# Moving relation gathers from the first pass of a graph network to the expert tiles that follow it

## The chip, the cores and the metric

One Trainium2 chip, one core. The time is the device time of one execution in microseconds (us). Each kernel is also profiled once; durations below come from that one profiled execution.

## The reference

Four blocks run one after the other on 3125 nodes of 256 features, in float32.

- Block 1 is a graph network of three layers. A layer takes, for every node, the mean over the edges that end in it (103125 edges, loops among them), multiplies by two weight matrices, and normalizes.
- Block 2 is a mixture of 16 experts. Each node picks its two best experts by a gate; an expert is relu(x w1 + b1) w2 + b2 with 512 hidden units, and the two answers are added to the node by their weights.
- Block 3 is a relational graph network: a message is the source's row times the row of the edge's relation. There are 500 relations, whose rows of 256 features carry a gate value as a 257th.
- Block 4 is a mixture of 8 experts with 1024 hidden units.

Only one thing of block 3 matters here: its relation rows depend on the edges' types alone, so they can be fetched in any earlier block.

## The kernel before

Nodes are held as 25 blocks of 128 (NB = 25). The edges of a block are sorted into 26 tiles of 128 edges, so there are 650 edge tiles in all.

**Pass 1** is the first layer of block 1, and it also sorts the edges. It is a loop of 28 steps (L640 to L662), each of which works on four blocks at different stages: `load` and `rank` of block i (the win loads on SP, L518, then a long chain between VectorE, DVE for short, and TensorE, PE: kb L528, prior L534, upto L542, place L546, ri L549), `permute` and `lay` of block i - 1 (held L593, main L605, the edge types into main_t L611), `build` of block i - 2 (one-hots L507, PE products, the store of cells on SP L637), and the sums (L359, L362) and `finish` of block i - 3. Passes 2 and 3 (from L848 and L873) are the second and third layers, which read the stored cells.

**The relation rows** of block 3 are fetched in advance from the 500-row table r_rows. `fetch_relations(n, after)` takes the next n of 217 groups of three edge tiles each (the last has two). For a group it does one small DVE operation (L296) that copies the types of its tiles into the tile paced and reads a piece of `after`, so that the group cannot start before that data is there; then three indirect DMAs of 128 rows of 257 numbers on POOL (L300) into a rel_rows tile, of which there are four; and it issues the store of the group before on SP (L311), into r_seq in HBM. Block 3 reads r_seq from there. The calls stand in this order:

- pass 1: at the end of `rank` (after qi, from the third block on), after `lay`, before `build` and after `finish`, one group each: 95 groups, 285 gathers
- pass 2 and pass 3: two groups in each of 25 steps, 100 groups
- ten groups ahead of block 2 (L1179), and the remaining twelve behind its expert tiles in the program's text (L1182), with beta as the data that they wait for. Since beta is there early, a scheduler that orders each engine's instructions has put nearly all of them ahead of the first tile.

**Block 2** is the function `moe` (L908 to L1170) with the tag f0. The routing part works out for each expert tile of 256 rows which nodes it takes (tok_g, tok_s), with which weight (wt_q) and by which expert (exp_i). Then 34 expert tiles run. Tile t reads its expert's number on SP (the value_load at L1100, 34 in all), loads w1_t and w2_t on SP (three buffers each), and has its 256 rows gathered by two indirect DMAs on POOL (xt, L249, issued two tiles ahead, eight buffers). PE transposes them (pt, L1110), multiplies by w1_t (ph, L1125), and after the activation (L1130 on DVE, L1134 on ScalarE) by w2_t (py, L1143). DVE scales (y, L1146, eight buffers), and two indirect DMAs on POOL add y to f0_total in HBM (L1148). At the end of tile t the function `beside(t)` of the caller is called; before, it adds beta to block t of xs.

Each engine runs its instructions in one order, and POOL and SP each issue their DMAs in that order: a gather or a store that waits holds what is behind it.

Of the kernel before, what the change touches and what calls it, by code (L numbers as in the profile page):

```python
# [40 lines left out]
I32 = mybir.dt.int32  # L41
# [9 lines left out]
NB = 25  # L51
# [22 lines left out]
def bcast(ap, n):  # L74

    return bass.AP(tensor=ap.tensor, offset=ap.offset, ap=[[0, P], [1, n]])
# [3 lines left out]
def gnn_moe_kernel(  # L80
# [9 lines left out]
    nc = tc.nc  # L90
# [27 lines left out]
    xs = const.tile([P, NB, D], F32, name="xs")  # L118
# [169 lines left out]
    def fetch_relations(n, after):  # L288

        for i in islice(next_r, n):
            g = of_group[i]
            rows = stage.tile([P, RG, W], F32, name="rel_rows")
            types = paced[:, g[0]:g[-1] + 1]
            nc.vector.scalar_tensor_tensor(  # L296
                types, after[:, :len(g)], 0, main_t[:, g[0]:g[-1] + 1],
                op0=ALU.bitwise_and, op1=ALU.bitwise_or)
            for j, t in enumerate(g):
                nc.gpsimd.indirect_dma_start(  # L300
                    out=rows[:, j, :], out_offset=None, in_=r_rows,
                    in_offset=bass.IndirectOffsetOnAxis(ap=types[:, j:j + 1], axis=0))
            store_relations()
            landing.append((i, rows))

    def store_relations():
        if not landing:
            return
        i, rows = landing.pop()
        n = len(of_group[i])  # L310
        nc.sync.dma_start(r_seq[i], rows[:, :n, :].rearrange("p r w -> p (r w)"))  # L311
# [10 lines left out]
    with ExitStack() as block:  # L322
# [30 lines left out]
        def sums_of(b, cell, layer, psum, between={}):  # L353


            width = D + 1 if layer == 0 else D
            z = psum.tile([P, D + 1], F32, name="z", bufs=2)
            for sh in range(NB):
                nc.tensor.matmul(z[:, :width], cell[:, sh, :], part_lo[:, sh, :width],  # L359
                                 start=sh == 0, stop=False)  # L360
                for i in range(2):
                    nc.tensor.matmul(z[:, :D], cell[:, sh, :], part_hi[:, sh, i, :],  # L362
                                     start=False, stop=sh == NB - 1 and i == 1)
                if sh in between:
                    between[sh]()
            return z

        def finish(b, z, layer):
            if layer == 0:
                nc.vector.tensor_copy(raw_dst[:, b:b + 1], z[:, D:])  # L370
                deg = work.tile([P, 1], F32, name="deg")
                nc.vector.tensor_scalar(deg, z[:, D:], 1.0, None, op0=ALU.max)
                nc.vector.reciprocal(inv_dst[:, b:b + 1], deg)
            zt = work.tile([P, D], F32, name="zt")
            nc.vector.scalar_tensor_tensor(zt, z[:, :D], inv_dst[:, b:b + 1], own[:, b, :],
                                           op0=ALU.mult, op1=ALU.add)
            if layer < 2:
                nc.vector.scalar_tensor_tensor(h[:, b, :], zt, 0.0, h[:, b, :],
                                               op0=ALU.max, op1=ALU.add)
            else:  # L380
                xt = work.tile([P, D], F32, name="xt")
                nc.scalar.dma_start(xt, base[b * P:(b + 1) * P, :])
                nc.vector.tensor_add(zt, zt, h[:, b, :])
                nc.vector.scalar_tensor_tensor(xs[:, b, :], zt, sound[:, 0:1], xt, op0=ALU.mult,
                                               op1=ALU.add)
            return zt

        with ExitStack() as first:
# [123 lines left out]
            def load(b):  # L512

                win = steps.tile([P, 6, 2, WH], F16, name="win", bufs=2)
                for half in range(2):
                    c = 2 * b + half
                    at_tile = nc.sync.value_load(begin[0:1, c:c + 1], min_val=0, max_val=ET - WH)
                    nc.sync.dma_start(win[:, :, half, :], words[:, :, bass.ds(at_tile, WH)])  # L518
                return win
# [47 lines left out]
            def permute(b, win, slot, to):  # L567


                def two(a):  # L570
                    return a.rearrange("p h (t two) -> p (h t) two", two=2)

                n = WH // 2
                all_of = [P, 2 * n, NS, 2]
                hit = steps.tile(all_of, F16, name="hit", bufs=1)
                nc.vector.tensor_tensor(
                    hit, two(to)[:, :, None, :].to_broadcast(all_of),
                    iota_tile[:, None, :, :].to_broadcast(all_of), op=ALU.is_equal)
                put = steps.tile([P, 2 * n, 3, NS, 2], F16, name="put")
                for i in range(3):  # L580
                    nc.vector.tensor_tensor(
                        put[:, :, i, :, :], hit,
                        two(win[:, 1 + i, :, :])[:, :, None, :].to_broadcast(all_of), op=ALU.mult)
                ends = psum.tile([P, 2, 3, NS], F32, name="ends")
                for half in range(2):
                    oh = one_hots(two(slot)[:, half * n:(half + 1) * n, :], n, iota_0, P,
                                  "oh_slot", n)
                    for t in range(WH):
                        nc.tensor.matmul(ends[:, half, :, :], oh[:, t // 2, :, t % 2],
                                         put[:, half * n + t // 2, :, :, t % 2],  # L590
                                         start=t == 0, stop=t == WH - 1)
                held = steps.tile([P, 3, NS, 2], F16, name="held")
                nc.scalar.activation(held, ends.rearrange("p h i t -> p i t h"), AF.Copy)  # L593


                for t in range(2):
                    nc.scalar.activation(held[:, :, b + t, 1], ends[:, 1, :, b + 1 - t], AF.Copy)
                return held
# [42 lines left out]
            def words_of(held):  # L641
                return held.rearrange("p i t h -> p (i t h)").bitcast(I32)

            loaded, ranked, moved, built = {}, {}, {}, {}
            for i in range(NB + 3):
                if i < NB:
                    loaded[i] = load(i)
                    ranked[i] = rank(i, loaded[i])
                if 0 <= i - 1 < NB:
                    moved[i - 1] = permute(i - 1, loaded.pop(i - 1), *ranked.pop(i - 1))  # L650
                    lay(i - 1, moved[i - 1])
                    if i > 1:
                        fetch_relations(1, words_of(moved[i - 1]))
                if 0 <= i - 2 < NB:
                    if i > 2:
                        fetch_relations(1, words_of(moved[i - 2]))
                    built[i - 2] = build(i - 2, moved.pop(i - 2))
                if 0 <= i - 3 < NB:
                    z = sums_of(i - 3, built.pop(i - 3), 0, psum)
                    done = finish(i - 3, z, 0)  # L660
                    if i > 3:
                        fetch_relations(1, done.bitcast(I32))  # L662

        with ExitStack() as flags:
            one = flags.enter_context(tc.tile_pool(name="g0_deg0", bufs=1))
# [16 lines left out]
        with ExitStack() as slow:  # L682
# [8 lines left out]
            with tc.For_i(0, n_slow, 1):  # L691
# [32 lines left out]
                for layer in range(3):  # L724
# [4 lines left out]
                    for b in range(NB):  # L729
# [3 lines left out]
                        z = psum.tile([P, D], F32, name="ps", bufs=3)  # L733
# [17 lines left out]
        with ExitStack() as later:  # L751
# [96 lines left out]
            for b, cell in enumerate(ahead_of(load_cell, 2)):  # L848
                z = sums_of(b, cell, 1, psum,
                            {12: lambda: fetch_relations(1, places(b, psum))})  # L850
# [3 lines left out]
                done = finish(b, z, 1)  # L854
# [20 lines left out]
            for b, cell in enumerate(ahead_of(load_cell, 2)):  # L875
                choice = chosen(b - 1)
                step = lambda: next(choice, None)
                z = sums_of(b, cell, 2, psum, {13: step, 19: step} if b > 0 else {})
                next(packs[b])
                done = finish(b, z, 2)  # L880
# [294 lines left out]
    with ExitStack() as block:  # L1175
        keep = block.enter_context(tc.tile_pool(name="f0_tokens", bufs=1))
        beta = keep.tile([P, D], F32, name="beta")
        nc.scalar.dma_start(beta, bcast(f0_beta, D))
        fetch_relations(10, top_v[:, NB - 1, :].bitcast(I32))  # L1179
        moe("f0", 16, 512, f0_b1, f0_w1, f0_w2, f0_b2, AF.Relu, None, f0_x, f0_total, 34,  # L1180
            lambda t: t < NB and nc.vector.tensor_add(xs[:, t, :], xs[:, t, :], beta))
        fetch_relations(len(of_group), beta.bitcast(I32))  # L1182
        store_relations()
    rel_ctx.close()
# [7 lines left out]
    with ExitStack() as block:  # L1192
# [14 lines left out]
        with ExitStack() as prep:  # L1207
# [6 lines left out]
            for kern, w, name in ((km, g1_mwt, "mw"), (ku, g1_uwt, "uw")):  # L1214
# [4 lines left out]
                for bo in range(4):  # L1219
                    for bi in range(4):  # L1220
                        i, sign = blades[bo][bi]
# [259 lines left out]
```

## Time and profile before

| what | value |
|---|---|
| runs | 3075.04, 3080.94, 3124.3 us; median 3080.94 |
| profiled execution, its own time | 3081.72 us |
| its span | 3079.8 us |
| mean granted TensorE clock | 0.910 |
| PE, DVE, ACT, POOL busy | 81%, 57%, 14%, 51% |
| pass 1 | about 155 to 681 us |
| routing of block 2 | 1341 to 1460 us |
| expert tiles of block 2 | 1460 to 1741 us |
| relation gathers (L300) | 650, of 0.943 to 3.072 us each, median 0.949 |

Times in the profile count from the start of the span. Engines: PE is the matrix engine, PEld its weight loads, DVE the vector engine, ACT the scalar engine, POOL the engine that issues the indirect DMAs, SP the one that issues the plain ones. An arrow (<-) names what an instruction waited for; "issue" is time in which an engine waited for nothing that the profile shows. A line number is that of the kernel before; in the changed kernel the lines from L660 on are two lower up to the end of `moe`, and somewhat higher behind it.

### The profile page before, as it was taken

How to read it: one execution, taken by the hardware profiler on the slowest of the kernel's cores; microseconds unless marked ns; L12 is line 12 of the kernel's file. 1: busy time of each engine (PE TensorE's matmuls, PEld its weight loads, DVE VectorE, ACT ScalarE, POOL GpSimd, SP SyncE). 2: the span in 40 equal slices, each digit the busy share in tenths (PEclk: the TensorE clock that was granted, in tenths of full speed). 3: DMA queues.
4: the chain of work that ended last, by engine and by line, in shares of the span. 5: the costliest groups of instructions: out<-in, count | busy, mean ns of one | idle time of the engine just before them, and what ended most of it. 6: DMA issues, size and time to landing. Idle time of an engine off the chain costs nothing.

```text
span 3079.8 us, 47955 instructions
## 1 busy us (share of the span) xinstructions
PE 2499.6 (81%) x17712; PEld 1986.2 (64%) x17712; DVE 1767.9 (57%) x4734; ACT 434.1 (14%) x1119; POOL 1566.1 (51%) x1379
## 2 busy tenths in 40 slices
PE   1767766778888999942999518999999996899997
PEld 0356654654777588832788406777777775788886
DVE  6688886766455366662233377788888787111110
ACT  1321221223000210000111050000000000122221
POOL 1067776761455256675566316666666660333331
PEclk9888897789999999976999859999999997899998
DMA  7046665652666368865777537777777770665653
GB/s 222 3 143 190 182 185 175 185 187 81 203 220 226 123 217 276 265 192 159 207 200 194 118 136 261 241 244 248 249 249 251 240 221 19 220 184 175 187 172 96
DMA packets 294160, 581.12 MB, mean 189 GB/s; under 512 B 77946, under 2 KB 176955, under 8 KB 289939
## 3 DMA queue, kind: packets, MB, share of 16 engines
q1 hardware_dynamic: 207459, 389.64, 36.9%
q0 software_dynamic: 76992, 177.86, 23.3%
q10 hardware_dynamic: 9456, 10.36, 1.1%
q8 instruction: 146, 2.39, 0.3%
q14 instruction: 107, 0.88, 0.1%
HBM read 433.05 MB, written 151.13 MB: 190 GB/s over the span
## 4 chain that ended last, share of the span: by engine, by line
PE 59%; DVE 15%; issue 7%; DMA 6%; another core or an unknown queue 5%; POOL 4%; ACT 1%; SPq 1%; POOLq 0%; DVEq 0%; ACTq 0%
PE ps L1414 12%; PE ph L1125 10%; PE py L1143 10%; PE hg_ps L1402 7%; PE z L362 5%; PE g L344 4%; POOL rel_rows L300 4%; PE z L359 2%; DVE oh_end L507 2%; DVE upto L539 2%; DMA cell<-cells 1%; PE pq L1043 1%; DMA rel_rows<-r_rows,paced 1%; DVE oh_slot L507 1%
## 5 line engine op out<-in xcount | busy, mean ns | idle before, releaser
L300 POOL DMA_INDIRECT rel_rows<-r_rows,paced x650 | 761.3, 1171 | 678.8 <-issue 158.6
L362 PE MATMUL z<-part_hi,cell 128*128 128x256 bf16 x3750 | 691.0, 285 | 23.9 <-issue 23.3
L359 PE MATMUL z<-part_lo,cell 128*128 128x256 bf16 (+1 forms) x1875 | 534.8, 285 | 18.4 <-issue 12.4
L1414 PE MATMUL ps<-prod,d_oh 128*128 128x257 f32 x1750 | 521.1, 392 | 26.5 <-issue 12.6
L362 PEld LDWEIGHTS <-cell 128*128 128x128 bf16 x3750 | 374.9, 102 | 85.0 <-issue 31.2
L1402 PE MATMUL hg_ps<-hc_part,s_oh 128*128 128x257 bf16 x1950 | 328.5, 275 | 98.0 <-DMA rg_seq<-r_seq 98.0
L1148 POOL DMA_INDIRECT f_total<-y,tok_s x126 | 198.3, 1574 | 354.0 <-DVE y L1146 275.3
L249 POOL DMA_INDIRECT hg<-hc_rows,spill_s x225 | 235.0, 1045 | 263.0 <-issue 125.9
L1143 PE MATMUL py<-w_t,hid 128*128 128x256 f32 x1472 | 335.1, 382 | 3.4 <-ACT hid L1134 3.4
L1125 PE MATMUL ph<-xT,w_t 128*128 128x256 f32 x1472 | 336.9, 386 | 0.8
L1405 DVE TENSOR_TENSOR prod<-hg_ps,rg_seq 128x257 f32<-128x257 f32 x650 | 270.4, 421 | 108.2 <-PE hg_ps L1402 65.2
L1414 PEld LDWEIGHTS ps<-prod,d_oh 128*128 128x128 f32 x1750 | 275.2, 191 | 81.5 <-issue 31.3
L1402 PEld LDWEIGHTS <-s_oh 128*128 128x128 bf16 x1950 | 191.6, 99 | 195.7 <-DVE s_oh L1358 98.4
L1146 DVE TENSOR_SCALAR y<-py,wt_q 128x256 f32<-128x256 f32 x126 | 61.0, 484 | 445.5 <-PE py L1143 440.8
L1125 PEld LDWEIGHTS ph<-xT,w_t 128*128 128x128 f32 x1472 | 280.4, 193 | 44.4 <-DVE xT L1115 3.7
L1143 PEld LDWEIGHTS py<-w_t,hid 128*128 128x128 f32 x1472 | 274.1, 191 | 50.8 <-ACT hid L1134 3.8
L249 POOL DMA_INDIRECT rg<-r_rows,spill_t x225 | 235.3, 1046 | 68.6 <-issue 68.6
L359 PEld LDWEIGHTS <-cell 128*128 128x128 bf16 x1875 | 192.5, 103 | 56.5 <-issue 23.1
L1134 ACT ACTIVATE hid<-ph,b_t 128x256 f32<-128x256 f32 x300 | 129.7, 471 | 647.8 <-PE ph L1125 524.8
L249 POOL DMA_INDIRECT xt<-f_x,tok_g x126 | 123.9, 983 | 99.0 <-DVE wt_q L1055 44.7
L507 DVE TENSOR_TENSOR oh_end<-held,iota 128x1024 bf16<-128x1024 f16 (+3 forms) x150 | 150.4, 1017 | 9.4 <-remote 5.0
L344 PE MATMUL g<-ww,hT 128*128 128x512 f32 x300 | 145.3, 629 | 8.2 <-ACT hT L143 8.0
(296 smaller groups left out, 2783.6 us busy)
## 6 DMA issues: line engine op xcount, KB each, us to landing
r_seq<-rel_rows SPq DMA_DIRECT2D x216, 385.5 KB
rg_seq<-r_seq SPq DMA_DIRECT2D x216, 385.5 KB
w_t<-in_L_ffn_W_dram SPq DMA_DIRECT2D x58, 1024.0 KB
cell<-cells SPq DMA_DIRECT2D x50, 800.0 KB
w_t<-in_L_ffn_w_dram SPq DMA_DIRECT2D x68, 512.0 KB
s_row<-main_s SPq DMA_DIRECT2D x25, 832.0 KB
cells<-cell SPq DMA_DIRECT2D x25, 800.0 KB
rel_rows<-r_rows,paced POOLq DMA_INDIRECT x650
```

Source lines behind the costliest of these rows:

```text
L249: nc.gpsimd.indirect_dma_start(out=rows, out_offset=None, in_=table, in_offset=bass.IndirectOffsetOnAxis(ap=ids, axis=0))
L300: nc.gpsimd.indirect_dma_start(out=rows[:, j, :], out_offset=None, in_=r_rows, in_offset=bass.IndirectOffsetOnAxis(ap=types[:, j:j + 1], a ...
L344: nc.tensor.matmul(g, hT[:, k, :], ww[:, layer, k, :], start=k == 0, stop=k == KD - 1)
L359: nc.tensor.matmul(z[:, :width], cell[:, sh, :], part_lo[:, sh, :width], start=sh == 0, stop=False)
L362: nc.tensor.matmul(z[:, :D], cell[:, sh, :], part_hi[:, sh, i, :], start=False, stop=sh == NB - 1 and i == 1)
L507: nc.vector.tensor_tensor(oh[:, :n, :, :], ids[:, :, None, :].to_broadcast([P, n, width, 2]), table[:, None, :width, :].to_broadcast([P, n ...
L1125: nc.tensor.matmul(ph[:, j - j0, :], w1_t[:, 0, k, j * P:(j + 1) * P], xT[:, k, :], start=k == 0, stop=k == KD - 1)
L1143: nc.tensor.matmul(py, hid[:, j, of], w2_t[:, 0, j, :], start=False, stop=j == nj - 1)
L1148: st = nc.gpsimd.indirect_dma_start(out=total, in_=y, in_offset=None, out_offset=bass.IndirectOffsetOnAxis(ap=tok_s[:, q:q + 1], axis=0), ...
L1402: nc.tensor.matmul(hg, s_oh[:, t, :], part[:, sh, i, :W], start=i == 2, stop=i == 0)
L1405: nc.vector.tensor_mul(prod, hg, rg)
L1414: nc.tensor.matmul(ps[b], d_oh, prod, start=is_first, stop=is_last)
```

## The change

In pass 1 the call behind `finish` goes. In block 2, `beside(t)` still adds beta to block t of xs, and for t below 25 it also fetches one group wherever t is not divisible by three: 16 groups. The 24 groups less in pass 1 (95 to 71) thus become 16 in `beside` and eight more in the call behind the tiles, which takes 20 instead of twelve.

```diff
                 if 0 <= i - 3 < NB:
                     z = sums_of(i - 3, built.pop(i - 3), 0, psum)
-                    done = finish(i - 3, z, 0)
-                    if i > 3:
-                        fetch_relations(1, done.bitcast(I32))
+                    finish(i - 3, z, 0)
...
+        def beside(t):
+            if t < NB:
+                nc.vector.tensor_add(xs[:, t, :], xs[:, t, :], beta)
+                fetch_relations(t % 3 > 0, xs[:, t, :].bitcast(I32))
+
         fetch_relations(10, top_v[:, NB - 1, :].bitcast(I32))
         moe("f0", 16, 512, f0_b1, f0_w1, f0_w2, f0_b2, AF.Relu, None, f0_x, f0_total, 34,
-            lambda t: t < NB and nc.vector.tensor_add(xs[:, t, :], xs[:, t, :], beta))
+            beside)
         fetch_relations(len(of_group), beta.bitcast(I32))
```

The data that a group in `beside` waits for is block t of xs after its addition. The code of `fetch_relations`, of `moe` and of block 3 is unchanged, and so is the set of rows that is fetched.

## The prediction

> **What bounds the kernel now.** I read the page first, for the busy engines, then the table of windows, because the change works in two stages, and in each the waits and the order in time.
>
> The page of the kernel before:
>
> ```profile
> span 3079.8 us, 47955 instructions
> PE 2499.6 (81%) x17712; PEld 1986.2 (64%) x17712; DVE 1767.9 (57%) x4734; ACT 434.1 (14%) x1119; POOL 1566.1 (51%) x1379
> L300 POOL DMA_INDIRECT rel_rows<-r_rows,paced x650 | 761.3, 1171 | 678.8 <-issue 158.6
> ```
>
> The gathers that move (L300) cost 1171 ns on average plus about 0.30 us of issue each. POOL has room over the whole span (51%); what counts is where the room lies. The windows (columns: length, PE, PEld, DVE, ACT and POOL busy, PE clock, DMA share, GB/s):
>
> ```profile
> 300.00:450.00 150.00, 110.41 (x1387) 89.46 (x1387) 124.14 (x276) 30.76 (x77) 110.96 (x82) 0.86 0.63 185
> 450.00:600.00 150.00, 104.27 (x1280) 84.07 (x1279) 113.13 (x253) 27.52 (x69) 106.44 (x80) 0.83 0.60 177
> 1350.00:1400.00 50.00, 13.94 (x55) 12.05 (x55) 30.02 (x96) 0.82 (x4) 39.02 (x37) 0.57 0.59 175
> 1400.00:1480.00 80.00, 25.86 (x94) 20.84 (x95) 14.81 (x37) 0.95 (x2) 39.48 (x41) 0.59 0.59 168
> 1480.00:1700.00 220.00, 219.44 (x1070) 186.13 (x1069) 74.30 (x171) 26.56 (x56) 138.67 (x108) 1.00 0.79 202
> ```
>
> Pass 1 (155 to 681 us) is a chain through the engines with DVE the fullest (124.14 of 150). The routing of block 2 (1341 to 1460) leaves PE nearly idle, and its expert tiles (1460 to 1741) fill PE (219.44 of 220). POOL's gathers between 351 and 511 us, and two rows of the waits of 200 to 650 us:
>
> ```profile
> L300 POOL DMA_INDIRECT rel_rows<-r_rows,paced x84 | 115.1, 1370 | 36.6 <-issue 21.9 <-DVE paced L296 5.3 <-DVE to L561 4.4
> DVE member L537 <- PE prior L534: 32.8, 11, 12.2
> DVE kb L528 <- DMA win<-edge_words: 10.6, 4, 4.9
> ```
>
> Here POOL has a backlog: 115.1 + 21.9 of 160 us, with hardly a wait on data. Its r_seq stores stand on SP ahead of the win loads, so DVE waits for win, 10.6 us in all. The other wait shown, prior, is the ordinary chain. The start of block 2 on POOL:
>
> ```profile
> 1402.42 0.95 POOL L300 DMA_INDIRECT rel_rows<-r_rows,paced  x1 [0.31 <-issue]
> 1423.14 0.95 POOL L300 DMA_INDIRECT rel_rows<-r_rows,paced  x1 [19.77 <-DMA r_seq<-rel_rows]
> ...
> 1453.22 0.95 POOL L300 DMA_INDIRECT rel_rows<-r_rows,paced  x1 [0.30 <-issue]
> 1454.47 0.95 POOL L249 DMA_INDIRECT xt<-f_x,tok_g  x1 [0.30 <-issue]
> ...
> 1468.27 0.95 POOL L300 DMA_INDIRECT rel_rows<-r_rows,paced  x1 [0.31 <-issue]
> 1478.29 1.63 POOL L1148 DMA_INDIRECT f_total<-y,tok_s  x1 [9.07 <-DVE y L1146]
> ```
>
> and on PE:
>
> ```profile
> 1460.29 0.67 PE L1110 MATMUL pt<-ident,xt 128*128 128x128 f32 x2 [38.78 <-DMA xt<-f_x,tok_g]
> ```
>
> PE waits 38.78 us for the first xt, and that xt stood behind relation gathers on POOL: one each 1.253 us, with a stop of 19.77 us while four rel_rows buffers waited for their stores. In the stop SP was loading the 34 expert numbers (1391.6 to 1419.3), ahead of the stores. So block 2 starts when POOL has worked off the gathers ahead of xt.
>
> **The change part by part.** All against the profiled execution, 3081.72 us (0.8 above the median of the runs shown, 3080.94). By the instruction order of the changed kernel, POOL has 213 gathers in pass 1 instead of 285, the same 294 in passes 2 and 3, 89 instead of 70 ahead of the first xt, and 54 instead of 1 after it, in packs of 7, 2, 10, 1, 10, 9, 2, 9 and so on among the first ten tiles or so. PE's order in block 2 and ACT's order are the same.
>
> *Pass 1, 24 groups fewer.* Step starts (held, L593) run from 155.17 to 661.39: 23 intervals, 22.0 us each; undisturbed intervals are 20.2 to 21.5, say 20.7. So irregular stalls come to 24 x 1.3 = 31 us. (a) 24 paced operations of 0.155 us leave DVE: 3.7 us. (b) POOL's work per step falls from 12 x (1.17 + 0.30) = 17.6 us, or 20.0 at the 1.37 of the backlog, to 9 x 1.67 = 15.0 at most, so the backlog goes, and with it the win waits: 10.6 us. SP loses one store of eight issues a step. What is late next is the chain over prior. (c) The other 20 us of stalls are late PE results that the trace gives no releaser for; between 0 and 20, I take 8, two fifths, since only some lie in the backlog. Sum -22. Low end of the gain: (a) may itself be hidden in DVE's waits, so 0; a loss is excluded, since nothing is added here. High end 3.7 + 31 = 35.
>
> *Passes 2 and 3.* 16 paced operations (0.15 us) enter DVE's third pass: 2.4 us, hidden under PE (230.57 of 250 busy, DVE 159.09). The 25 additions of beta are as before. Zero; 2.4 if the cover is gone.
>
> *Start of block 2.* 19 more gathers ahead of xt: 19 x 1.253 = 23.8 us. But SP's order has the 34 loads woven between stores of r_seq 180 to 195, where before they stood in one block; so the stop of 19.8 goes. Net +4; +24 if it stays; -16 is out, since the 89 gathers need 111.5 us of POOL from 1341.6, to 1453.1 at the least with the iotas.
>
> *Expert tiles.* A tile takes PE 7.83 us (three in 23.5) and POOL 2 x (0.98 + 0.30) + 2 x (1.57 + 0.30) = 6.3 us: 1.5 us of room. 54 gathers x 1.253 = 67.7 us come in, against 9.1 us of idle time before the first y and 10 x 1.53 = 15.3 us of room in ten tiles: 43 us do not fit. They stand ahead of later xt gathers and y scatters on POOL; with two tiles of xt ahead and eight y buffers, PE is stopped from about the seventh tile on and never gets it back, for it is full to the end. Following the queues by hand gives 40 us; I take 41. On SP the stores of r_seq 196 to 216, each waiting for its gather, now stand between the weight loads of tiles 4 to 10. What is behind them waits too, but mostly in the same 41 us.
>
> *The DMA engines there.* Between 1460 and 1560 they are 77% busy: 13.76 MB in 41.4 us of hardware queue, 6.51 MB in 35.1 us of software queue. 54 gathers and their stores are 7.1 MB each way: 7.1/6.51 x 35.1 = 38 us and 7.1/13.76 x 41.4 = 21 us. Ten tiles' own 60 us and these 59 make 119 in a stretch of 78 + 41 = 119 us: just full. Landings (3.7 us now for a gather, 4 for weights) get later: from 0 up to 20 us, I take 7.
>
> Sum: -22 + 0 + 4 + 41 + 7 = +30: 3111.7, say **3112 us**.
>
> One rule against this: the Trainium skill, page "SBUF — State Buffer", section "SBUF: two separate sides", says that a VectorE operation in its two-port mode locks GpSimd out, which then cannot write descriptors. The rows show 1370 ns a gather in busy pass 1, 950 in the route, and 986 for an xt gather among the tiles, where DVE is a third busy with float32 work. By the rule the moved gathers might cost 1.67 us with issue, the sum then going to about 3143; the row says 1.25 to 1.29, and I go by the row.
>
> **The rivals.**
> 1. *Slower by over 2%: gathers in the tiles as dear as in pass 1.* 73 gathers (19 + 54) at 1.67 instead of 1.253 are 30.5 us more: 3142. Each further 0.1 us is 7.3. For it: the full DMA engines, and 1.37 us where DMA was at 0.63 only. Against: 986 ns of the xt gathers at 0.79. It decides from 1.68 us a gather; at 2.0 us 3166.
> 2. *The cover holds in block 2.* If xt is far enough ahead and the gathers fill only POOL's idle time: tiles and DMA cost some 10 instead of 48: 3074. For it: POOL is 63% busy there. Against: 138.67 + 0.30 a piece leaves no 68 us in ten tiles.
> 3. *Pass 1 gives all its stalls.* -35 instead of -22: 3099, still within 2%. For it: POOL without wait from 351 to 511. Against: late PE results also at 218 and 610, away from the backlog. Faster than 3019 would need this and a free block 2 and 28 us more.
>
> That the change does not do what it says is excluded by the instruction order.
>
> **How the numbers follow.** My forecast (3095 to 3135) 0.45, rival 1 0.28 (3142 and above; lowering pass 1 to a gain of 0 lifts the forecast to 3134), rival 2 0.13, rival 3 0.09, both of the last 0.05. From the ends, 3066 to 3165 leaves out some 2 in 10: it takes rivals 2 and 3 in, and rival 1 up to 2.0 us a gather. The 2% bounds, about what a measurement can tell from no change, are 3019.3 and 3142.6: faster 0.05, same 0.67, slower 0.28.
>
> **What would show it.** Pass 1: mean step 21.0 to 21.2 us, no win wait, POOL waiting on DVE in every step. Start: first xt near 1432 to 1440 of the new span (18 earlier by pass 1 less 22 plus 4), no stop of some 20 us for r_seq. Tiles: PE idle 40 to 50 us in sum between the sixth and the eleventh tile, released by xt or w_t DMAs, then 7.83 us a tile again. Wrong: PE at 100% throughout (rival 2), L300 over 1.4 us among the tiles (rival 1), or steps still at 22 us, which would say that the backlog was not the cause of the stalls.

## The result and the profile after

The changed kernel takes 3123.5 us, the median of four runs from 3103.5 to 3146.9, where the kernel before takes 3080.0 (four runs, one more than were shown above). The ratio is 1.013 with a 95% interval of 1.008 to 1.018: slower by a little over one per cent, on the forecast's side (3112) and inside its range. The profiled execution took 3131.87 us, 8 above that median, so its stages are to be compared with some care.

The first lines of the page, and the row of the moved gathers:

```profile
span 3130.1 us, 47959 instructions
PE 2512.6 (80%) x17712; PEld 1990.7 (64%) x17712; DVE 1767.7 (56%) x4734; ACT 432.8 (14%) x1119; POOL 1565.1 (50%) x1379
L300 POOL DMA_INDIRECT rel_rows<-r_rows,paced x650 | 763.3, 1174 | 694.2 <-DVE paced L296 179.1
```

Little shows here: the engines do the same work in 50 us more, and PE is busy 13 us longer for as many matmuls. The stages show it. The table is made from times in the two traces: the start of the first and of the last held of pass 1, the end of the last z of pass 3, the start of the first and the end of the last ph of block 2, the same of ps in block 3, and the last y that is added in block 4.

| stage, us | before | after | difference | forecast |
|---|---|---|---|---|
| pass 1, first to last held | 511.7 | 463.3 | -48.4 | -22 |
| to the last z of pass 3 | 675.6 | 681.0 | +5.4 | 0 |
| to the first ph of block 2 | 126.8 | 140.0 | +13.2 | +4 |
| to the last ph | 270.9 | 341.4 | +70.5 | +48 |
| to the first ps of block 3 | 102.9 | 102.8 | -0.1 | 0 |
| to the last ps | 724.2 | 734.0 | +9.8 | 0 |
| to the last y of block 4 | 499.2 | 498.4 | -0.8 | 0 |

So both halves of the forecast have the right sign and both are too small. The windows of pass 1, and then of the expert tiles (columns as before):

```profile
300.00:450.00 150.00, 115.61 (x1462) 93.78 (x1459) 126.29 (x275) 34.69 (x85) 92.94 (x68) 0.89 0.56 165
450.00:600.00 150.00, 118.62 (x1502) 97.00 (x1502) 134.44 (x289) 31.11 (x77) 98.63 (x69) 0.89 0.58 171
```

```profile
1434.80:1480.00 45.20, 35.70 (x141) 28.37 (x141) 8.83 (x20) 3.79 (x8) 27.82 (x25) 0.84 0.66 191
1480.00:1530.00 50.00, 22.42 (x75) 17.08 (x74) 5.52 (x13) 1.89 (x4) 33.28 (x33) 0.66 0.68 188
1530.00:1590.00 60.00, 39.46 (x156) 31.81 (x155) 10.41 (x24) 3.68 (x8) 38.40 (x35) 0.77 0.76 197
1590.00:1776.20 186.20, 185.56 (x903) 157.16 (x902) 62.45 (x143) 22.24 (x47) 112.43 (x86) 1.00 0.76 186
```

In pass 1 DVE rises to 134.44 of 150 with fewer gathers beside it. In the tiles PE is full only from 1590 us on, when the moved gathers (the last at 1558.7 us) and their stores are done. Before that it is idle for 57 us in 155, and the granted clock falls to 0.66. In the waits of 200 to 650 us, POOL now waits for data, while the wait for win, which the forecast wanted to see go, is longer than before (19.6 instead of 10.6):

```profile
POOL rel_rows L300 <- DVE paced L296: 62.4, 11, 12.3
DVE member L537 <- PE prior L534: 19.8, 10, 6.2
DVE kb L528 <- DMA win<-edge_words: 19.6, 7, 4.6
```

The two traces from the first chip, before and after, and below those of group 3, hold only about half as many records of landed transfers as those of groups 1 and 2 (8 for each transfer instead of 16). In them a wait that a transfer ended can stand under another name or under none.

At the start of block 2 the stop for r_seq has shrunk from 19.77 to 4.29 us, and the gathers ahead of xt run on to 1423.65:

```profile
1402.17 0.94 POOL L300 DMA_INDIRECT rel_rows<-r_rows,paced  x1 [4.29 <-DMA r_seq<-rel_rows]
...
1422.40 0.94 POOL L300 DMA_INDIRECT rel_rows<-r_rows,paced  x1 [0.30 <-issue]
1423.65 0.95 POOL L249 DMA_INDIRECT xt<-f_x,tok_g  x1 [0.30 <-issue]
```

### The profile page after: what moved, and what is told of

Read it like the earlier page. It is cut to its first block, busy times and chain, and to the rows that moved or that the text cites. A ratio compares the mean times of both kernels' runs of the same rounds, so it can differ in the third digit from the quotient of the medians.

```text
span 3130.1 us, 47959 instructions
## 1 busy us (share of the span) xinstructions
PE 2512.6 (80%) x17712; PEld 1990.7 (64%) x17712; DVE 1767.7 (56%) x4734; ACT 432.8 (14%) x1119; POOL 1565.1 (50%) x1379
## 4 chain that ended last, share of the span: by engine, by line
PE 54%; DVE 7%; issue 5%; DMA 5%; another core or an unknown queue 4%; POOL 2%; ACT 1%; SPq 0%; DVEq 0%; ACTq 0%; POOLq 0%
PE ps L1418 11%; PE ph L1123 10%; PE py L1141 10%; PE hg_ps L1406 6%; PE z L362 5%; PE g L344 3%; PE z L359 3%; POOL rel_rows L300 2%; PE pt L141 1%; DVE prod L1409 1%; DMA f_total<-y,tok_s 1%; DMA cell<-cells 1%; PE pt L1108 1%; DMA rel_rows<-r_rows,paced 1%
## 5 line engine op out<-in xcount | busy, mean ns | idle before, releaser
L1141 PE MATMUL py<-w_t,hid 128*128 128x256 f32 x1472 | 347.5, 391 | 53.5 <-ACT hid L1132 31.1
L1141 PEld LDWEIGHTS py<-w_t,hid 128*128 128x128 f32 x1472 | 280.8, 196 | 106.2 <-ACT hid L1132 33.1
```

Of the source, the lines that this page charges most:

```text
L1141: nc.tensor.matmul(py, hid[:, j, of], w2_t[:, 0, j, :], start=False, stop=j == nj - 1)
```

## The experiments

Each group of four ran on one chip, and the kernel before took 2964, 2967 and 3136 us on the three: chips differ by several per cent. Ratios are to the kernel before on the same chip. That kernel was timed on the three chips, but not profiled there, so stages are compared within a group or between the first two groups, which agree. The diffs are excerpts; where rows are not fetched or not stored, block 3 reads other rows in their place.

**Group 1: the parts by themselves.** `p1_alone` has pass 1 as changed; the 24 groups are left out.

```diff
-    next_r = iter(range(len(of_group)))
+    next_r = iter(range(len(of_group) - 24))
...
-                    done = finish(i - 3, z, 0)
-                    if i > 3:
-                        fetch_relations(1, done.bitcast(I32))
+                    finish(i - 3, z, 0)
```

> Pass 1 with three groups in each step, as in the changed kernel; the 24 groups that leave it are not fetched at all, and block 3 reads the last fetched group in their place. Block 2 has the twelve groups behind it of the kernel before. Theory A (pass 1's gain is real and comes from fewer gathers there): pass 1 from the first to the last held lasts 463 us as in the changed kernel, 48 less than before, the start of block 2 and its tiles take what they took before, total 3025 to 3040. Theory B (half of the 48 us was the luck of one execution, the forecast's 22 was right): pass 1 lasts 485 to 490, total 3055 to 3065.

Measured: 0.990 (0.987 to 0.993), 2936 us, 28 less. `b2_alone` has pass 1 as before and block 2 as changed:

```diff
-    next_r = iter(range(len(of_group)))
+    next_r = iter([*range(len(of_group)), *range(24)])
...
+                fetch_relations(t % 3 > 0, xs[:, t, :].bitcast(I32))
...
-        fetch_relations(len(of_group), beta.bitcast(I32))
+        fetch_relations(len(of_group) + 24, beta.bitcast(I32))
```

> Block 2 with one group in two of three tiles and 20 behind, as in the changed kernel, but pass 1 as before with four groups; the number of groups is kept up by fetching the first 24 a second time. Theory A (the changed block 2 costs what its trace shows, start +11, tiles +71, and some 10 in block 3): 3080 + 82 to 92 = 3162 to 3172. Theory B (POOL's time that does not fit, as forecast: +4 and +48): 3080 + 52 = 3132.

Measured: 1.0215 (1.019 to 1.024), 3028 us, 64 more: between the two theories (82 to 92, and 52). `p1_alone` and `b2_alone` come from one chip, so their difference in pass 1 is that of four and three groups: 474.4 and 442.8 us, a gain of 31.6. Their tiles differ by 315.3 - 265.2 = 50.1, and the way to the first ph by 133.9 - 122.5 = 11.4. Block 3 takes 683.7 and 684.8: the 9.8 us of the first traces do not come back here, so they are not put down to the change. The gain too lies between its theories: part of the 48 us belonged to the first chip or execution, and 22 was too low. POOL's gathers in 150 to 590 us, first `b2_alone`, then `p1_alone`:

```profile
L300 POOL DMA_INDIRECT rel_rows<-r_rows,paced x240 | 350.3, 1459 | 231.0 <-DMA main_s<-rows_sb 153.0 <-issue 62.5 <-DVE paced L296 4.2
```

```profile
L300 POOL DMA_INDIRECT rel_rows<-r_rows,paced x200 | 315.2, 1576 | 267.0 <-DMA main_s<-rows_sb 152.5 <-DVE paced L296 59.0 <-issue 49.7
```

The 153 us are the time before the first gather. With four groups POOL is busy or issuing for 350.3 + 62.5 = 413 us of the 427 that follow: it sets the pace of pass 1. With three it waits 59 us for DVE, and DVE is busy 402 of the 440 us instead of 376.

`no_store_b2` is the changed kernel without the stores of the last 36 groups:

```diff
         i, rows = landing.pop()
+        if i > 180:
+            return
```

> The changed kernel without the r_seq stores of the last 36 groups (those fetched from block 2 on); block 3 reads one earlier group in their place. POOL has the same number of gathers, SP has no store among the weight loads. Theory A (the tiles lose 71 instead of 41 us because weight loads stand behind stores on SP, which wait for gathers, which wait on POOL behind y scatters, which wait for PE): PE's idle time among the tiles falls from about 76 to 40 to 45, total 3085 to 3095. Theory B (POOL alone holds PE): idle time as in the changed kernel, total 3115 to 3130.

Measured: 1.014 (1.010 to 1.017), 2999 us. The scheduler moves gathers when the stores are gone: 100 stand ahead of the first xt instead of 89, so the start took 145.0 us, and 43 behind instead of 54. The tiles took 304.9 us, 40 above `p1_alone` instead of 50, so theory A falls as it was put: most of the loss stays. What PE waited for is below, with `after_again`.

`spread` puts the 24 groups into passes 2 and 3 (the edit in pass 3 is the same); pass 1 is as in the changed kernel, block 2 as before:

```diff
                 done = finish(b, z, 1)
-                fetch_relations(1, done.bitcast(I32))
+                fetch_relations(1 + b % 2, done.bitcast(I32))
```

> Three groups in each step of pass 1, the 24 others one each in every second step of passes 2 and 3, block 2 as before. Theory A (POOL and SP have room in passes 2 and 3, where PE is the bound): 3080 - 48 + 0 to 10 = 3032 to 3042. Theory B (passes 2 and 3 are no better a cover than the tiles; 72 gathers at 1.25 us come to 90): 3080 or more.

Measured: 1.020 (1.017 to 1.024), 3018 us: theory B. Pass 1 keeps its gain (443.7), but from there to the last z the time is 717.5 us instead of 648.1 in `p1_alone`: 69 us for 72 gathers. A wait that grows is that of DVE for the stored cells, in `p1_alone` and in `spread` (660 to 1240 us):

```profile
DVE some_src L850 <- DMA cell<-cells: 110.2, 21, 11.2
```

```profile
DVE some_src L850 <- DMA cell<-cells: 151.9, 21, 13.8
```

**Group 2: what in pass 1 costs the time.** `p1_no_store` is the kernel before without the stores of the 24 groups behind finish, `p1_paced_only` also without their gathers (its edit is shown; `p1_no_store` leaves out the store alone):

```diff
+            if skip:
+                skipped.add(i)
+                continue
             rows = stage.tile([P, RG, W], F32, name="rel_rows")
...
-                        fetch_relations(1, done.bitcast(I32))
+                        fetch_relations(1, done.bitcast(I32), True)
```

> The kernel before, without the r_seq stores of the 24 groups fetched behind finish in pass 1 (block 3 reads the group before in their place); their paced operations and gathers stay. Held to held, pass 1 took 474 us with four groups and 443 with three on the chip of the first four runs. Theory A (SP: a store ahead of the win loads and cells stores holds them): pass 1 within 8 us of the three-group kernel of this call. Theory B (POOL: twelve gathers a step are too many): pass 1 as with four groups, 25 to 32 us above the three-group kernel.

> The kernel before, with only the paced operation left of the 24 groups behind finish in pass 1: no gathers and no stores for them (block 3 reads the group before in their place). Theory A (the gathers, with or without the stores, make up the gain): pass 1 at the three-group kernel plus 24 x 0.155 = 4 us. Theory B (the DVE operation and its wait on the end of finish hold up DVE's order): 15 us or more above it.

Measured: `p1_no_store` 0.998 (0.996 to 1.0005), pass 1 470.9 us; `p1_paced_only` 0.988 (0.985 to 0.990), pass 1 442.5 us; the three groups of `after_again` on this chip 441.1 us. So the paced operations are worth 1.4 us, the 24 stores next to nothing while the gathers stay (470.9 against the 474.4 of `b2_alone`), and the gathers make up the gain of 30. They do not make DVE's own operations dearer: from 150 to 590 us these take 380.6 us for 848 in `p1_no_store` and 404.0 us for 898 in `p1_paced_only`, 0.45 us each. DVE's wait for win shows how they act, in `p1_no_store` and then in `p1_paced_only` (150 to 590 us):

```profile
DVE kb L533 <- DMA win<-edge_words: 57.2, 18, 5.4
```

```profile
DVE kb L532 <- DMA win<-edge_words: 32.6, 17, 4.0
```

With the backlog the wait is 57 us even without a quarter of the stores (61.5 in `b2_alone`); the other three stores of a step still wait for a POOL that is behind, which is the likely reason. Without the backlog it is 32 to 35 us, in all kernels with three groups on these two chips. A fall of 25 to 29 us is nearly the whole gain. (`p1_paced_only` is 39 us below the kernel before in all; 14 of them lie in passes 2 and 3, 633.7 us against 647.7 in `p1_no_store`, for a reason that was not looked into.)

`after_again` is the changed kernel unchanged.

> The changed kernel, unchanged, as the measure for this call's chip. Theory A (b2_alone and p1_alone add up: +62 in block 2 and its start, -28 in pass 1): ratio 1.010 to 1.014. Theory B (the two parts are not independent): outside 1.005 to 1.02.

Measured: 1.011 (1.009 to 1.0125), 2999 against 2967 us, 32 more: the parts add up. Against `p1_no_store`, which has block 2 as before, the way to the first ph is 134.6 - 123.0 = 12 us longer and the tiles 312.7 - 263.2 = 49.5; against that, pass 1 is 30 shorter. PE's waits in the tiles of `after_again` (1371.9 to 1684.5 us), then SP's wait in the same stretch, then PE's in `no_store_b2` (1381.8 to 1686.7):

```profile
PE py L1141 <- DMA w_t<-in_L_ffn_w_dram: 28.2, 4, 9.6
PE pt L1108 <- DMA xt<-f_x,tok_g: 5.6, 6, 2.9
PE ph L1123 <- DMA w_t<-in_L_ffn_w_dram: 4.8, 2, 3.3
```

```profile
SPq L311 <- DMA rel_rows<-r_rows,paced: 81.5, 20, 7.5
```

```profile
PE pt L1110 <- DMA xt<-f_x,tok_g: 32.1, 8, 17.4
```

PE waits 33.0 us for weights and 5.6 for xt. The weights are late because SP stands 81.5 us at stores whose gathers have not landed. They also land later: by the trace's records of semaphores, a weight load takes 6.6 us from issue to landing (median) from 1372 to 1500 us in `after_again` and 6.1 in the same stretch of `b2_alone`, against 4.5 in `p1_no_store` and 4.1 in `p1_alone`, which have block 2 as before. How the 33.0 us divide between the two was not measured. Take the stores away, and the loads land after 4.4 us again, but PE waits 32.1 us for xt instead: POOL would hold it for nearly as long. The two limits stand one behind the other, and neither is worth much alone.

`behind24` fetches the rest behind the last y, and keeps 22 groups ahead of block 2:

```diff
+        def beside(t, y):
+            if t < NB:
+                nc.vector.tensor_add(xs[:, t, :], xs[:, t, :], beta)
+            if t == 33:
+                fetch_relations(len(of_group), y.bitcast(I32))
```

> Three groups a step in pass 1; 22 groups ahead of block 2; the rest paced by the last y of block 2, so that 66 gathers run after the last expert tile, where 95 us pass on the trace before block 3's first sum and POOL is nearly idle. Theory A (that stretch covers them): pass 1's 28 to 32 us are kept, ratio 0.985 to 0.993 to the kernel before. Theory B (relation gathers and stores cost about 1 us each wherever SP issues other loads, as in passes 2 and 3, since a store that waits for its gathers holds SP): +40, ratio 1.01 or more.

Measured: 1.010 (1.008 to 1.012), 2997 us. Pass 1 (443.8) and the tiles (263.5) are as good as they get, but from the last ph to block 3's first sum 169.5 us pass instead of 103 to 110. The waits of 1630 to 1850 us name one reason:

```profile
DVE rs_main L1201 <- DMA r_seq<-rel_rows: 51.0, 1, 51.0
```

The first tile of block 3 lies where the relation buffers were, so DVE cannot begin until the last store is done.

**Group 3: other places.** All three have three groups in pass 1, the relation buffers on the other side of the memory until block 3's loop, and groups in the tiles that are paced by the tile's own y.

```diff
-    stage = rel_ctx.enter_context(tc.tile_pool(name="rel_stage", bufs=4))
+    stage = rel_ctx.enter_context(tc.tile_pool(name="rel_stage", bufs=4, side="right"))
...
+            fetch_relations(len(of_group) if t == 33 else t % 3 == 1, y.bitcast(I32))
```

That is `third_side`; `two_thirds_y` has `t < NB and t % 3 > 0` in the last line, and `ten_side` is `third_side` with 10 groups ahead of block 2 instead of 22.

> The same 16 groups in two of three tiles below 25, but each paced by the y of its own tile instead of by a block of xs that is ready long before; 22 groups ahead of block 2 as before, the last 8 paced by the last y, and the relation buffers kept apart from block 3's memory until they are done. Theory A (the loss in the tiles comes from all 48 gathers piling up in the first ten tiles, where 15 us of POOL's room are): spread over 25 tiles they meet 16 x 3.76 = 60 us of work with 38 us of room, so the tiles (first to last ph) take 265 + 10 to 25 us instead of 312 to 315. Theory B (each gather among the tiles costs PE about 0.9 us wherever it stands, through DMA and SP): 265 + 43 or more.

> As two_thirds_y, but one group in each third tile only (11 groups), and 13 behind the last y. Theory A: 3.76 us of gathers in three tiles fit into 3 x 1.53 = 4.6 us of room, so the tiles take 265 to 270 us; the 39 gathers behind take 49 us of the 95 in which POOL has nothing to do, so nothing is lost there; ratio 0.985 to 0.992, from pass 1's 28 to 39 us. Theory B (the stores on SP hold the loads of block 3's start as in behind24): from the last y to block 3's first sum 115 us or more instead of 95, ratio 0.995 to 1.005.

> As third_side, with 10 groups ahead of block 2 instead of 22 and 25 behind the last y: 36 gathers fewer ahead of the first xt. Theory A (block 2 starts when POOL has worked off the gathers ahead of xt): from the last z of pass 3 to the first ph 85 to 100 us instead of 122, and 75 gathers in 94 us behind just fit; ratio 0.975 to 0.985. Theory B (they come back behind: 45 us more work in a stretch that other work fills): ratio as third_side or higher.

Measured: 1.001 (0.998 to 1.0045), 1.001 (0.998 to 1.004) and 1.000 (0.996 to 1.003): none is faster than the kernel before, so whatever pass 1 gained is given back. How much that was on this chip is not known, as no kernel with four groups was profiled there. The tiles took 314.7, 303.7 and 300.5 us, where theory A had 275 to 290 and 265 to 270; with block 2 as before they take 264.3 on this chip (`spread_act`, below). Behind them 116, 136 and 170 us passed to block 3's first sum, for 8, 13 and 25 groups, against 100 there. (The profiled execution of `third_side` took 21 us more than its median, so its stages are rough.) `ten_side` starts block 2 as expected, 96.4 us after the last z, since POOL waits for the routing and no longer works off gathers:

```profile
1380.69 0.94 POOL L249 DMA_INDIRECT xt<-f_x,tok_g  x1 [29.17 <-DVE wt_q L1053]
```

It loses these 30 us behind the tiles (170 us instead of 136). In `third_side` the gathers fit into POOL's room, and PE is stopped all the same, here once in three tiles. SP, then PE, in 1595 to 1630 us:

```profile
1596.94 1.39 SPq L1100 DMA_DIRECT2D w_t<-in_L_ffn_w_dram  x1
1618.96 0.33 SPq L311 DMA_DIRECT2D r_seq<-rel_rows  x1
1619.88 0.04 SPq L1103 DMA_DIRECT2D w_t<-in_L_ffn_w_dram  x1
```

```profile
1625.95 3.63 PE L1141 MATMUL py<-w_t,hid 128*128 128x256 f32 x8 [3.23 <-DMA w_t<-in_L_ffn_w_dram]
```

SP issues nothing for 20 us, because the next instruction is a store that waits for the gathers, which wait for y. The weight load right behind it is late, and PE waits for weights 26.2 us in eight places. No stop of these tiles stands ahead of pt, which needs xt, so here the queue of SP does it, and not POOL's backlog.

`spread_act` takes the stores off SP in passes 2 and 3:

```diff
-        nc.sync.dma_start(r_seq[i], rows[:, :n, :].rearrange("p r w -> p (r w)"))
+        (nc.scalar if i > 70 else nc.sync).dma_start(r_seq[i], rows[:, :n, :].rearrange("p r w -> p (r w)"))
```

> The kernel spread (one group more in every second step of passes 2 and 3) with the r_seq stores from pass 2 on issued by ACT's queue instead of SP's. Theory A (passes 2 and 3 got 70 us longer since stores that wait for their gathers stand ahead of the cell loads on SP): passes 2 and 3 fall from 718 us to 650 or less, and the DVE wait for cell goes. Theory B (the gathers' own traffic and POOL time): 700 or more. ACT waiting for gathers ahead of its own work may take some of the gain back in both.

Measured: 1.039 (1.033 to 1.045); from pass 1's end to the last z 861.6 us, where the other three of this chip take 681 to 698 us. It does not settle the question, as the wait moved to ACT, whose own work it holds:

```profile
ACT rT L143 <- DMA rel_rows<-r_rows,paced: 145.3, 21, 7.7
```

No kernel that does the whole work beat the kernel before.

## Why the prediction was right, step by step

**Pass 1, 24 groups fewer: right mechanism, mis-sized.** POOL's backlog was the cause: 30 to 32 us go with the gathers. On the chips of groups 1 and 2 they go where term (b) put them, in the wait for win, but that wait falls by 25 to 29 us instead of the 10.6 that the first trace showed, and does not end: 32 to 35 us of it stay. On the first chip the trace shows it the other way about: the named win wait grew by 9 us, and the gain of 48 us, beyond the high end of 35, stands under the stalls of term (c), of which I took 8 of 20. There ACT's wait for held had 35.5 us without a named releaser, which are gone after. As these two traces lack half the landings, the 10.6 us that sized term (b) are not safe either, and the cause of the stalls on the first chip stays open.

**Passes 2 and 3: right within 5 us**: +5.4 between the first two traces, +5 between `p1_alone` and `b2_alone`, 0 between `p1_no_store` and `after_again`. `spread` shows that gathers with their stores are not free there.

**Start of block 2: mis-sized, 11 to 13 instead of 4.** The 19 gathers cost 22 to 25 us, as forecast (23.8). What was mis-sized is the stop that goes. On the first chip POOL's waits for r_seq ahead of the first xt fell from 19.8 to 5.8 us (the longest left is the 4.29 above), not to 0. On the chips of groups 1 and 2 they had been only 12 us (`p1_alone`, `p1_no_store`) and fell to 3 (`b2_alone`, `after_again`). So 14 us went on the first chip, and 9 to 10 on the others, instead of 19.8, which leaves about what was measured.

**Expert tiles and the DMA engines: 41 + 7 = 48 against 49.5 and 50.1 on two chips**, and 70.5 in the first trace. The size was right, the reason half. The forecast had PE stopped by xt behind POOL and held the waits on SP for hidden "in the same 41 us". It was the other way about: the weights behind SP's stores ended last, and POOL's backlog was the one hidden behind them. That both are close in size is why the number came out. All this is read from the chips of groups 1 and 2. In the first trace PE's stops end with ACT's hid, and ACT's own waits there stand in part under no name (53.3 us "remote", 39.9 us "issue" in 1434 to 1777 us); where the 20 us by which its tiles exceed the others' come from stays open.

The 7 us of the DMA term are not seen by themselves. The DMA engines were busy 0.87 of the time in `after_again` from 1425 to 1500 us, and the weights landed 2 us later, as above; what that cost lies inside PE's waits. In the place of the 7 us stands something that the forecast left out, the clock. PE was stopped for 36 to 39 us more than with block 2 as before, and was itself busy 11 to 14 us longer with the same matmuls (273.3 us in `after_again` against 262.4 in `p1_no_store`, 276.7 in `b2_alone` against 262.6 in `p1_alone`), at a granted clock of 0.94 instead of 1.00. Of the 70.5 us of the first trace, 16.5 are of this kind: 283.1 us busy after, 266.6 before.

**The sum is in part luck.** On the second group's chip the parts are -30, +12 and +49.5, in all +32 where +30 was forecast: 8 us too little gain in pass 1 and 8 us too little loss at the start of block 2 cancel.

**Rival 1** falls: the gathers among the tiles cost 952 ns, as the rows of before said; the dearer gather that was weighed there did not come. **Rival 2** falls: the tiles cost 49.5 to 70.5 us, not some 10. **Rival 3** has its condition fulfilled on the first chip (48 us, more than its 35), but a dearer block 2 came with it, and its 3099 did not.

## What to carry to other kernels

Before work is moved to an engine with idle time, look at what is issued behind it on every queue: a store that waits for the moved transfer holds all loads behind it on its queue, even where the engine that does the transfer has room (`third_side`). A stop of PE also costs clock: here 11 to 16.5 us beyond the stops. Data that is ready early paces nothing: sixteen groups meant for 25 tiles were all issued in the first ten. When two waits lie one behind the other, taking one away shows the other (`after_again` and `no_store_b2`), so price both before expecting a gain.

## What the runs showed of the hardware

A gather was dearer where DVE was busier: 0.95 us among the tiles (DVE busy 16% from 1434.8 to 1590 us), 1.37 in the backlog of the kernel before (80 to 83%), 1.46 in `b2_alone` (376 of 440 us, 85%), 1.58 in `p1_alone` (402 of 440, 91%). Fewer gathers in pass 1 thus got dearer, by 0.12 us between the last two, although the DMA engines were less busy there (0.58 against 0.64). That DVE is the cause was not tested. The direction is that of the Trainium skill, page "SBUF — State Buffer", section "SBUF: two separate sides", where DVE can lock GpSimd out; no run here measured the lock itself.

PE's stops cost more than their length. The matmuls of L1141 in the changed kernel from 1434 to 1590 us, then from 1600 to 1770:

```profile
L1141 PE MATMUL py<-w_t,hid 128*128 128x256 f32 x153 | 50.7, 493 | 53.5 <-ACT hid L1132 31.1 <-issue 22.4
```

```profile
L1141 PE MATMUL py<-w_t,hid 128*128 128x256 f32 x346 | 80.0, 381 | 0.0
```

They take 493 instead of 381 ns on average where the stops are, with a granted clock of 0.66 to 0.84 instead of 1.00. The Trainium skill, page "TensorE: Matmul & The Clock Gate", section "What's actually happening", says that the clock falls to half after an idle window of about 3.4 us; the stops here were up to 15.8 us, and the rows agree.
